# A four-layer vision stack on one core: a separate tile for the second product of the output projection, another order at the beginning and the end, and norms of both token blocks side by side

## The chip, the core and the metric

The kernel runs on one core of a Trainium2 chip. The core has a matrix engine (TensorE, PE in the profile, with weight loads as PEld), a vector engine (VectorE, DVE), an activation engine (ScalarE, ACT), GpSimd (POOL) and SyncE (SP), which issues the transfers. The metric is device time in microseconds, the median of several runs. All data are 32-bit floats.

## The reference

The input has 4 images of 512 channels and 32x32 pixels, 1024 tokens each. Four layers follow each other:

```python
# layer 0: attention with 8 heads of 64, residual
qkv = xs @ Wp.T + bp;  attn = softmax(q k * 64**-0.5);  x = res @ Wo.T + bo + xs
# layer 1: linear attention with softplus features, residual
wval = Qf (Kf^T V) * norm;  x = x + gamma * wval
# layer 2: LayerNorm over the channels of each token, attention with one head of 512, residual
xn = (xf - mu) * rsqrt(var + 1e-5) * norm_w;  x = x + (softmax(q k * 512**-0.5) v) w_proj + b_proj
# layer 3: GroupNorm, attention with 4 heads of 128, residual
```

The mean and the variance of layer 2 are taken for each token over its 512 channels.

## The kernel before

**Layout.** An image (in the code "batch" b) lies as x with channels on the 128 partitions, in 4 chunks c, and tokens along the free dimension, in two blocks tb of 512. A 128x128 by 128x512 product appears as two records of PE in the trace, and as two weight loads. Products go to accumulation tiles `acc` (4 buffers of one bank) or to `two_tile` (2 buffers of two banks).

**Strassen-like products.** `seven_products` computes a 2x2 block product with seven instead of eight block products p1 to p7 (Winograd's form). It needs four sums of the inputs (`sum_inputs`, on VectorE) and four sums of the weights (`sum_weights`, on GpSimd, L704 to L707: s[0] first, then s[1], which reads s[0], s[2], and s[3], which reads s[1]). p6 uses s[1], p7 uses s[2], p5 uses s[0], p3 uses s[3]; p1 and p2 need no sums. In each group of outputs they run in the order p1, p1, p2, p2, then p6, p7, p6, p5, p4, p7, p3, p5, p4, p3.

**Who calls `sum_weights`.** `block_sums` (tile `ws` of 128x256 operands, for the query and key projections), `project_v` (tile `ws` of 128x512 operands, from the weights `w` or `wqkv`), `output_sums` (tile `os`), and layer 2 itself, for the score product of its single head: there the "weights" are the queries (L1815, tile `qs`, 128x1024 operands, the fourth sum written over `q`). In layer 2 the program calls it for `qs` first, then calls `project_v`, then `one_head`, which uses `qs`.

**Order on the engines.** The order of PE is the order of the program (`manual_schedule`, L1673). A scheduler sets the order of the other engines from its own model of when things are ready, with some links written out: `tc.issue_after(i)` puts an instruction behind another one in the order, `soon()` raises a priority. Each engine runs its own queue in order. `pieces` is a list of small jobs of a neighbouring layer or batch that are put between products, one per `slot()`; `idle` is an empty job, which leaves one slot for something to come ready. `later` holds jobs that come due after some steps of attention.

**Output projection.** `project_out` (L1071) is a seven-product form too, over half a token block. Its first product goes into tile ps[1], ScalarE copies it to d (L1112, tile `ou`), and the second product accumulates on the same tile, so that it waits for the copy. `finish` adds the tile to x (L1101), and in the last layer stores it. Parts `second`, `third` and `fourth` are due with some steps in between in layer 0 and one right after another in layer 3.

**LayerNorm.** `layer_norm` (L1563) for one token block: `add` sums the four chunks of x on VectorE to a row tile; `center` multiplies it with a 128x128 matrix of ones (L1580, so that each partition holds the sum), subtracts the mean from four chunks (L1582), squares on ScalarE and adds (L1591); `spread` multiplies the squares with ones (L1596), takes the root and the reciprocal (L1599); `scale` multiplies the four chunks (L1604). For batches 2 and 3 both blocks are done in the previous batch of layer 2 (L1817), in slots of `project_v` and `one_head`.

**Beginning and end.** The first transfers are x and the query weights chunk by chunk, then the key weights, the second token block, the value weights (L586 to L593). In the last projection, `end_program` (L1135), the products of three of four chunks are made for all four outputs, then the verdict on the range of the denominators (`end()`, L1661), then the last chunk for outputs 0, 2, 1, 3, each added to x and stored (L1065).

## Time and profile before

| | us |
|---|---|
| median of 3 runs | 2415.14 (2414.91 to 2416.72) |
| profiled execution | 2416.26 |
| its span | 2414.5 |
| PE busy | 2398.0 (99%) |
| VectorE busy | 1503.3 (62%) |
| ScalarE busy | 702.0 (29%) |
| GpSimd busy | 247.8 (10%) |
| transfers | 110.15 MB, mean 46 GB/s |

Layer 0 with layer 1 in its slots runs to about 906 us, layer 2 to about 1566, layer 3 to the end. In the views, a line of the timeline gives start, duration, engine, line of the code, operation, output and input tiles, shapes and count, and in brackets the idle time before it with what ended it. A line of the waits gives who waited for whom, the sum in us, the number of waits and the longest. The duration of a single PE record is that of a pipelined product; the distance between starts is what it costs.

### The profile page before, as it was taken

How to read it: one execution, taken by the hardware profiler on the slowest of the kernel's cores; microseconds unless marked ns; L12 is line 12 of the kernel's file. 1: busy time of each engine (PE TensorE's matmuls, PEld its weight loads, DVE VectorE, ACT ScalarE, POOL GpSimd, SP SyncE). 2: the span in 40 equal slices, each digit the busy share in tenths (PEclk: the TensorE clock that was granted, in tenths of full speed). 3: DMA queues.
4: the chain of work that ended last, by engine and by line, in shares of the span. 5: the costliest groups of instructions: out<-in, count | busy, mean ns of one | idle time of the engine just before them, and what ended most of it. 6: DMA issues, size and time to landing. Idle time of an engine off the chain costs nothing.

```text
span 2414.5 us, 24620 instructions
## 1 busy us (share of the span) xinstructions
PE 2398.0 (99%) x10002; PEld 1197.7 (50%) x10002; DVE 1503.3 (62%) x1820; ACT 702.0 (29%) x866; POOL 247.8 (10%) x240
## 2 busy tenths in 40 slices
PE   9999999999999999999999999999999999999999
PEld 4544534453445344544646445455556446455653
DVE  4578577757875789695676765654463554445344
ACT  1454154415531653230302202013221330331132
POOL 4001100110020001102102020111020001002000
PEclk9999999999999999999999999999999999999999
DMA  5001220212021213112001020110010001001001
GB/s 188 2 18 36 57 80 11 61 31 80 19 62 64 99 37 104 64 54 78 1 9 70 13 87 0 61 70 18 35 70 0 23 31 53 0 35 35 0 26 41
DMA packets 44485, 110.15 MB, mean 46 GB/s; under 512 B 3687, under 2 KB 19559, under 8 KB 41422
## 3 DMA queue, kind: packets, MB, share of 16 engines
q1 hardware_dynamic: 44366, 108.52, 13.4%
q8 instruction: 80, 1.31, 0.2%
q14 instruction: 39, 0.32, 0.0%
HBM read 73.69 MB, written 33.77 MB: 45 GB/s over the span
## 4 chain that ended last, share of the span: by engine, by line
PE 97%; DVE 2%; ACT 0%; issue 0%; DMA 0%; SPq 0%; DVEq 0%; ACTq 0%
PE acc L716 19%; PE acc L841 12%; PE acc L976 9%; PE acc L991 9%; PE sc L945 9%; PE sc L940 9%; PE acc L1299 8%; PE acc L848 8%; PE acc L1093 7%; PE acc L1027 1%; PE upd L1534 1%; PE acc L1465 1%; PE feat L1389 0%; PE out L1141 0%; PE feat L650 0%; PE kv L1514 0%
## 5 line engine op out<-in xcount | busy, mean ns | idle before, releaser
L950 ACT ACTIVATE pt<-sc 128x1024 f32<-128x1024 f32 x384 | 379.6, 1022 | 531.6 <-PE sc L945 304.1
L959 DVE TENSOR_TENSOR sum<-sum,pt 128x1024 f32<-128x1024 f32 x256 | 314.5, 1229 | 159.6 <-ACT pt L950 147.0
L976 PE MATMUL acc<-pt,v 64*64 64x512 f32 x2048 | 245.7, 591 | 0.0
L940 PE MATMUL sc<-q,k 64*64 64x512 f32 x2048 | 243.8, 591 | 1.1 <-ACT pt L950 1.1
L991 PE MATMUL acc<-pt,v 128*128 128x512 f32 x512 | 240.8, 594 | 0.0
L945 PE MATMUL sc<-q,k 128*128 128x512 f32 x512 | 239.8, 593 | 0.0
L716 PE MATMUL acc<-t,ws 128*128 128x512 f32 x384 | 173.9, 593 | 0.0
L704 POOL TENSOR_TENSOR ws<-wqkv 128x256 f32<-128x256 f32 (+1 forms) x40 | 39.3, 982 | 1294.2 <-PE acc L1027 513.3
L956 DVE TENSOR_TENSOR sum<-pt 128x1024 f32<-128x1024 f32 x64 | 78.0, 1219 | 137.4 <-ACT pt L950 137.4
L991 PEld LDWEIGHTS acc<-pt,v 128*128 128x128 f32 x512 | 96.6, 190 | 125.3 <-issue 121.6
L945 PEld LDWEIGHTS sc<-q,k 128*128 128x128 f32 x512 | 96.8, 190 | 116.2 <-issue 92.9
L976 PEld LDWEIGHTS acc<-pt,v 64*64 64x64 f32 x2048 | 76.7, 133 | 144.0 <-issue 141.2
L940 PEld LDWEIGHTS sc<-q,k 64*64 64x64 f32 x2048 | 76.3, 133 | 141.8 <-issue 133.0
L716 PEld LDWEIGHTS acc<-t,ws 128*128 128x128 f32 x384 | 72.7, 190 | 88.0 <-issue 87.5
L755 ACT COPY v<-acc 128x512 f32<-128x512 f32 x24 | 14.1, 586 | 305.1 <-PE acc L841 305.1
L687 DVE RECIPROCAL rd<-acc 128x512 f32<-128x512 f32 (+1 forms) x25 | 83.8, 3353 | 29.1 <-PE acc L1027 29.1
L1093 PE MATMUL acc<-ot,wo 128*128 128x256 f32 x360 | 86.7, 383 | 4.1 <-ACT ou L1112 3.4
L755 ACT COPY q<-acc 128x512 f32<-128x512 f32 x40 | 23.5, 586 | 223.6 <-PE acc L716 223.6
L841 PE MATMUL acc<-ws,t 128*128 128x256 f32 x384 | 87.1, 380 | 0.0
L848 PE MATMUL acc<-qs,w 128*128 128x512 f32 x192 | 86.5, 592 | 0.0
L848 PE MATMUL acc<-q,ln 128*128 128x512 f32 x192 | 86.4, 593 | 0.0
L1093 PEld LDWEIGHTS acc<-ot,wo 128*128 128x128 f32 x360 | 67.2, 190 | 28.8 <-issue 10.3
(307 smaller groups left out, 3375.6 us busy)
## 6 DMA issues: line engine op xcount, KB each, us to landing
home<-x SPq DMA_DIRECT2D x8, 2048.0 KB
x<-home SPq DMA_DIRECT2D x8, 2048.0 KB
rds<-quotients SPq DMA_DIRECT2D x32, 256.0 KB
squares<-squares SPq DMA_DIRECT2D x32, 256.0 KB
out<-x SPq DMA_DIRECT2D x32, 256.0 KB
rds<-quotients SPq DMA_DIRECT2D x7, 1024.0 KB
x<-in_x SPq DMA_DIRECT2D x3, 2048.0 KB
v<-squares SPq DMA_DIRECT2D x12, 512.0 KB
```

What stands on the lines that cost most here:

```text
L687: nc.vector.reciprocal(rd, ps)
L716: nc.tensor.matmul(ps, lhsT=w[:, m, :], rhs=x[:, m, :], start=start, stop=stop, skip_group_check=True)
L841: nc.tensor.matmul(ps[:, bass.ts(r, C // 2)], lhsT=x[:, m, bass.ts(2 * o + r, P)], rhs=w[:, m, :], start=(start and r == 0), stop=stop, sk ...
L848: nc.tensor.matmul(ps, lhsT=x[:, m, bass.ts(o, P)], rhs=w[:, m, :], start=start, stop=stop, skip_group_check=True,)
L940: nc.tensor.matmul(ps[half(h), s, :], lhsT=key(g, i)[half(s), half(h)], rhs=q[qb][half(s), g, :], start=True, stop=True,)
L945: nc.tensor.matmul(ps[:, s, :], lhsT=key(g, 2 * i + s), rhs=q[qb][:, g, :], start=True, stop=True)
L950: exps.append(nc.scalar.activation(pt, ps, AF.Exp, scale=scale).ins)
L959: adds.append(nc.vector.tensor_tensor(acc, acc, pt, ALU.add).ins)
L976: nc.tensor.matmul(outs[qb, g][r][half(s), :], lhsT=v[i // 2][half(r), i % 2, g * P + s * hd : g * P + (s + 1) * hd], rhs=pt[half(r), s, : ...
L991: nc.tensor.matmul(outs[qb, g][0], lhsT=v[j // 2][:, j % 2, bass.ts(g, P)], rhs=pt[:, s, :], start=(j == 0), stop=(j == NT - 1),)
L1093: nc.tensor.matmul(ps[i][:, bass.ts(o, n)], lhsT=w[:, m, bass.ts(o, P)], rhs=t[:, m, :], start=(start and m + o == 0), stop=(stop and m == ...
L1299: nc.tensor.matmul(ps[i, o], lhsT=w[m][:, bass.ts(o, P)], rhs=t[m], start=(start and m == 0), stop=(stop and m == 3), skip_group_check=True,)
```

## The change

Six things change. (1) The first query weights come in two transfers, the first of 128 columns; the second token block comes before the key weights, and these in two halves. (2) Six products of the ones matrix with itself stand first in the order of PE, into a tile that nothing reads. (3) In `sum_weights` the first sum is put behind the second sum of the call before (`seconds`), and the third behind the second of its own. (4) The second product of `project_out` gets a tile of its own, ps[2]; `finish` adds that and d to x. (5) In `end_program` the first three chunks are multiplied for outputs 0 and 2 alone before the verdict, then the last chunk of these, then outputs 1 and 3 whole; the last output is added and stored in halves. (6) For batches 2 and 3, `layer_norm_pair` takes the place of two `layer_norm`: the sums of both blocks are made by products with 32 columns of ones, into rows 0 to 31 and 32 to 63 of one tile, ScalarE scales them (or takes the root, with one reciprocal for both), and two transfers by way of DRAM spread the two rows over the partitions; the mean is then added from memory and not from the product's tile.

```diff
--- before.py
+++ after.py
@@ -585,11 +585,15 @@
     x_tile(0)
     for c in range(NC):
         nc.sync.dma_start(xs[0][:, c, :TB], xin[0, :, c, :TB])
-        nc.sync.dma_start(wqkv0[:, c, :C], wview[:, c, :C])
+        for o in ((0, P), (P, C)) if c == 0 else ((0, C),):
+            nc.sync.dma_start(wqkv0[:, c, slice(*o)], wview[:, c, slice(*o)])
     cols = const.tile([P, NCOLS], F32, name="cols")
     nc.sync.dma_start(cols, d["cols"])
-    nc.sync.dma_start(wqkv0[:, :, C : 2 * C], wview[:, :, C : 2 * C])
     nc.sync.dma_start(xs[0][:, :, TB:], xin[0, :, :, TB:])
+    for o in ((C, C + 2 * P), (C + 2 * P, 2 * C)):
+        nc.sync.dma_start(wqkv0[:, :, slice(*o)], wview[:, :, slice(*o)])
     nc.sync.dma_start(wqkv0[:, :, 2 * C :], wview[:, :, 2 * C :])
     loaded0 = load_bias(d["bv0"], d["wo0n"], v_tiles()[:2])
     wo0 = load_wo(d["wo0"])
@@ -657,6 +661,8 @@
     joined, summed = [], []
+    seconds = []
     def tick():
         for item in later:
             item[0] -= 1
@@ -701,9 +707,12 @@
     def sum_weights(s, w):
-        nc.gpsimd.tensor_tensor(s[0], w(1, 0), w(1, 1), ALU.add)
-        nc.gpsimd.tensor_tensor(s[1], s[0], w(0, 0), ALU.subtract)
-        nc.gpsimd.tensor_tensor(s[2], w(0, 0), w(1, 0), ALU.subtract)
+        with tc.issue_after(seconds[-1]) if seconds else nullcontext():
+            nc.gpsimd.tensor_tensor(s[0], w(1, 0), w(1, 1), ALU.add)
+        seconds[:] = [nc.gpsimd.tensor_tensor(s[1], s[0], w(0, 0), ALU.subtract).ins]
+        with tc.issue_after(seconds[0]):
+            nc.gpsimd.tensor_tensor(s[2], w(0, 0), w(1, 0), ALU.subtract)
         nc.gpsimd.tensor_tensor(s[3], w(0, 1), s[1], ALU.subtract)
         return s
@@ -1062,12 +1071,6 @@
             with tc.issue_after(exps[-1]):
                 nc.scalar.activation(xv, xv, AF.Identity, bias=bo[:, g : g + 1])
-        def finish(qb, o, ps):
-            xv = x[:, o, bass.ts(qb, TB)]
-            nc.vector.tensor_tensor(xv, ps, xv, ALU.add)
-            if last:
-                nc.sync.dma_start(xout[b, :, o, bass.ts(qb, TB)], xv)
         def project_out(qb):
@@ -1108,13 +1111,14 @@
                         xv(i, tb),
                     )
-            mult(1, w(0, 0), inputs(0, 0), stop=False)
+            mult(1, w(0, 0), inputs(0, 0))
             nc.scalar.copy(d, view(ps[1]))
             sum_inputs(t, inputs)
             def second():
-                mult(1, w(0, 1), inputs(1, 0), start=False)
-                finish(0, 0, 1, xv(0, 0))
+                mult(2, w(0, 1), inputs(1, 0))
+                finish(0, 0, 2, xv(0, 0), d)
                 mult(6, os[1], t[1])
                 add(6, d)
@@ -1136,20 +1140,32 @@
             ot = ots.pop(qb)
             two = [two_tile("out") for _ in range(NC // 2)]
-            for o in range(NC):
-                for c in range(NC - 1):
+            def mult(o, cs):
+                ps = two[o // 2][:, o % 2, :]
+                for c in cs:
                     nc.tensor.matmul(
-                        two[o // 2][:, o % 2, :], lhsT=wo[:, c, bass.ts(o, P)], rhs=ot[:, c, :],
-                        start=(c == 0), stop=False,
+                        ps, lhsT=wo[:, c, bass.ts(o, P)], rhs=ot[:, c, :],
+                        start=(c == 0), stop=(c == NC - 1),
                     )
+                if c < NC - 1:
+                    return
+                n = 2 if o == NC - 1 else 1
+                for h in range(n):
+                    ts = bass.ts(h, TB // n)
+                    xv = x[:, o, qb * TB : (qb + 1) * TB][:, ts]
+                    nc.vector.tensor_tensor(xv, ps[:, ts], xv, ALU.add)
+                    nc.sync.dma_start(xout[b, :, o, qb * TB : (qb + 1) * TB][:, ts], xv)
+            early, late = range(NC - 1), (NC - 1,)
+            mult(0, early)
+            mult(2, early)
             end()
-            for o in sorted(range(NC), key=lambda o: o % 2):
-                ps = two[o // 2][:, o % 2, :]
-                nc.tensor.matmul(
-                    ps, lhsT=wo[:, NC - 1, bass.ts(o, P)], rhs=ot[:, NC - 1, :],
-                    start=False, stop=True,
-                )
-                finish(qb, o, ps)
+            mult(0, late)
+            mult(2, late)
+            mult(1, range(NC))
+            mult(3, range(NC))
@@ -1607,6 +1623,72 @@
         return [add, center, spread, scale]
+    def layer_norm_pair(b, tiles):
+        t = {"sq": []}
+        x = lambda tb, c: xs[b][:, c, bass.ts(tb, TB)]
+        n = P // 4
+        def add():
+            t["s"] = [row_tile("s") for _ in range(NTB)]
+            for tb, s in enumerate(t["s"]):
+                nc.vector.tensor_tensor(s, x(tb, 0), x(tb, 1), ALU.add)
+                for c in range(2, NC):
+                    nc.vector.tensor_tensor(s, s, x(tb, c), ALU.add)
+            t["all"] = work.tile([P, NC, TB], F32, tag="rds", name="norms")
+        def sums(parts):
+            ps = two_tile("lnsums")[:, 0, :]
+            for tb, s in enumerate(parts):
+                nc.tensor.matmul(
+                    ps[tb * n : (tb + 1) * n, :], lhsT=ones[:, :n], rhs=s, start=True, stop=True
+                )
+            return ps[: NTB * n], row_tile("lnrow")[: NTB * n]
+        def spread(i, row):
+            home = dram.tile([NTB, TB], F32, tag="norms", bufs=2, name="norms")
+            nc.sync.dma_start(home, row[0 : NTB * n : n])
+            nc.sync.dma_start(t["all"][:, i : i + NTB, :], home.partition_broadcast(P))
+        def means():
+            ps, row = sums(t.pop("s"))
+            nc.scalar.activation(row, ps, AF.Copy, scale=-1.0 / C)
+            spread(0, row)
+        def center(tb):
+            xn = tiles[tb]
+            for c in range(NC):
+                nc.vector.tensor_tensor(xn[:, c, :], x(tb, c), t["all"][:, tb, :], ALU.add)
+            for c in range(NC):
+                sq = row_tile("sq")
+                nc.scalar.activation(sq, xn[:, c, :], AF.Square)
+                if c == 0:
+                    t["sq"].append(sq)
+                else:
+                    nc.vector.tensor_tensor(t["sq"][tb], t["sq"][tb], sq, ALU.add)
+        def deviations():
+            ps, row = sums(t.pop("sq"))
+            nc.scalar.activation(row, ps, AF.Sqrt, bias=eps[: NTB * n], scale=1.0 / C)
+            nc.vector.reciprocal(row, row)
+            spread(NTB, row)
+        def scale(tb):
+            for c in range(NC):
+                v = tiles[tb][:, c, :]
+                nc.vector.scalar_tensor_tensor(
+                    v, v, col("nw2", c), t["all"][:, NTB + tb, :], ALU.mult, ALU.mult
+                )
+        return [
+            add, means, lambda: center(0), lambda: center(1), deviations,
+            lambda: scale(0), lambda: scale(1),
+        ]
     affine = {}
@@ -1671,6 +1753,12 @@
     with tc.manual_schedule(engines={mybir.EngineType.PE}):
+        ps = acc_tile()
+        for _ in range(6):
+            nc.tensor.matmul(ps[:, :P], lhsT=ones, rhs=ones, start=True, stop=True)
         bo0 = []
@@ -1814,9 +1902,9 @@
             places = [halves[:, 0], halves[:, 1], third, pair(q[1], 0)]
             sum_weights(places, lambda i, j: pair(q[i], j))
             if 0 < b < B - 1:
-                (add0, *n0), (add1, *n1) = [layer_norm(b + 1, tb, after) for tb in range(NTB)]
+                norm = layer_norm_pair(b + 1, after)
                 pieces.extend([
-                    add0, n0[0], idle, n0[1], n0[2], add1, n1[0], idle, n1[1], n1[2],
+                    norm[0], idle, norm[1], idle, idle, *norm[2:4], idle, norm[4], idle, idle, *norm[5:],
                 ])
             elif b > 0:
                 first = chunks_tile("ot", "gn")
```

In the built program, the order of PE differs only at these places. That of VectorE differs where instructions were added or removed, and in the first part of layer 2. The order of GpSimd differs throughout.

## The prediction

> **What bounds the kernel now.** I read the page first (busy times), then the waits of TensorE, then the timeline of each place that the change touches. The page says that TensorE is busy nearly all the time, and the waits say how little there is to win:

> ```profile
> PE 2398.0 (99%) x10002; PEld 1197.7 (50%) x10002; DVE 1503.3 (62%) x1820; ACT 702.0 (29%) x866; POOL 247.8 (10%) x240
> ...
> PE acc L716 <- DMA wqkv<-in_wqkv: 4.7, 1, 4.7
> PE acc L1093 <- ACT ou L1112: 3.4, 5, 0.7
> PE sc L940 <- ACT pt L950: 1.1, 4, 0.3
> PE acc L1093 <- DVE ot L1060: 0.7, 1, 0.7
> ```

> All waits together are 10.4 us; the last product ends at 2408.5 us, and 6.0 us of tail follow. So any instruction taken from TensorE counts in full, and any operand that becomes late counts in full. The beginning is also slow: the weight load before 9.88 us takes 0.34 us, those after it 0.19 us.

> ```profile
> 9.10 0.34 PEld L716 LDWEIGHTS acc<-x,wqkv 128*128 128x128 f32 x1 [0.52 <-issue]
> 9.88 0.19 PEld L716 LDWEIGHTS acc<-x,wqkv 128*128 128x128 f32 x1 [0.45 <-issue]
> ```

> The 32 records of L716 from 4.70 to 21.04 us take 16.3 us, where 32 x 0.429 = 13.7 is the later pace: 2.6 us are lost to a slow clock. The windows at the end show the clock falling again (columns: length of the stretch; busy time and count of PE, PEld, DVE, ACT, POOL; granted clock; share of DMA; GB/s):

> ```profile
> 2411.00:2412.00 1.00, 0.00 (x0) 0.00 (x0) 0.00 (x0) 0.00 (x0) 0.00 (x0) 1.00 0.14 43
> 2412.60:2412.80 0.20, 0.00 (x0) 0.00 (x0) 0.00 (x0) 0.00 (x0) 0.00 (x0) 0.95 0.00 0
> 2412.80:2413.00 0.20, 0.00 (x0) 0.00 (x0) 0.00 (x0) 0.00 (x0) 0.00 (x0) 0.50 0.32 82
> ```

> It drops from 1.00 to 0.50 at about 2412.8, 4.3 us after the last product.

> The place that decides is layer 2. Timeline of GpSimd (start, duration) and of TensorE in batch 1:

> ```profile
> 1124.22 1.72 POOL L704 TENSOR_TENSOR ws<-w 128x512 f32<-128x512 f32 x1
> ...
> 1127.12 1.27 POOL L705 TENSOR_TENSOR ws<-ws,w 128x512 f32<-128x512 f32 x1
> ...
> 1146.66 2.35 POOL L704 TENSOR_TENSOR qs<-q 128x1024 f32<-128x1024 f32 x1 [16.93 <-DVE q L748]
> 1148.96 2.35 POOL L706 TENSOR_TENSOR qs<-q,q 128x1024 f32<-128x1024 f32 x1
> 1151.27 2.35 POOL L705 TENSOR_TENSOR qs<-qs,q 128x1024 f32<-128x1024 f32 x1
> ...
> 1145.63 7.07 PE L841 MATMUL acc<-w,ln 128*128 128x256 f32 x32
> 1152.53 1.02 PE L1580 MATMUL lnsums<-s,ones 128*128 128x512 f32 x2
> ```

> The value projection starts at 1145.63 and wants its weight sums `ws` at 1152.5; they were made at 1124 to 1130, long before. The sums `qs` of the queries, wanted only by the scores after it, are made at 1146.66 to 1156.1, when the last query is joined.

> **The change part by part.** The sum is made against the profiled execution's own 2416.26 us (span 2414.5), which is 1.1 us above the median, 2415.14. 0.2% is 4.8 us, about what a measurement of this kernel can tell from no change.

> *Order of the weight sums.* `sum_weights` now ties its first instruction behind the second one of the call before it. In the code the call for `qs` stands before the one in `project_v`, so in the built program GpSimd runs, in each batch of layer 2: `qs` first, second, third, `ws` first, `q` fourth, `ws` second, third, fourth. The hoist of `ws` to 1124 is gone. TensorE's product with the second `ws` (p6) waits for it, and everything stands behind that in its queue. From the start-to-start times of the rows: 2.4 + 2.3 + 2.3 for three `qs`, 1.2 for `ws` first, 2.3 for `q`, 1.3 for `ws` second, 0.1 for the signal, together 11.9 us after the join. Batch 1: 1146.66 + 11.9 = 1158.6 against 1152.5, a stall of 6.1. Batch 2: 1295.61 + 11.9 against 1301.45, 6.1. Batch 3: 1444.56 + 11.9 against 1450.6, 5.9. Batch 0 has pieces of layer 1 ahead of p6 (996.74): 985.41 + 11.9, 0.6. Together +18.7. The third sum follows 1.3 later, before p7 needs it 1.7 later. Bounds: 17.5 with rows 2% shorter; 22 if every `ws` row takes 1.72, as one did beside a busy VectorE. In layers 0 and 3 the new order costs nothing: `ws` then waits for block sums 2 and 3, but 14 products, over 20 us, lie between these and p6.

> *The clock in these stalls.* Three stalls of 6 us outlast the 4.3 us after which the clock fell at the end, and at the beginning it took 5.2 us of work to return. Upper bound: 5.2 us at half pace, 2.6 each, 7.7 in all; lower bound 0, if it doesn't fall. The stall passes the 4.3 us by only 1.8, and both delays are single samples, so I take a little over half: +4.5. [...]

> *Beginning.* The first weights are 64 KB instead of 256: at the 358 GB/s of the stretch from 3 to 4 us that is up to 0.5 us off the first wait, at least 0 (the input is as large as before): -0.25. Six 128x128 products of `ones` run from 1.2 us. They are 12 records of 0.21 (a quarter of the 0.855 us spacing) to 0.34 (a weight load each), so they end at 3.8 to 5.3, at worst 0.6 us past the old start. If the clock rises 5.2 us after the first work, at 6.4, the real products from 4.45 lose 1.0 instead of 2.6: -1.6. Bounds -2.6 and 0, with +0.6 for the late end. [...] The second token block now loads before the key columns, and these come in halves: first half at about 14.3 (the third megabyte was in at 12.9, the fourth at 15.6), two sums of 0.73 to 1.7 on GpSimd, 17.7 at the latest; TensorE needs them at 4.45 + 13.7 + 1.0 = 19.2. Nothing. SP issues two more transfers, 0.5 us each, before loads that have 2 us or more in hand.

> *Second product in its own tile.* Four of the five 3.4 us waits on L1112 (the copy of `ou`, one in each batch of layer 3) go: 4 x 0.68 = -2.7. Next late would be `oi` (L696), done at 1710.3 where the product would reach it at 1715.2: covered. The fifth, at 919.6, goes but the product then waits for `ot` (L1060) until 922.1 as before: 0. The new addition of `d`, 15 x 0.6 us on VectorE, lies in its idle gaps of about 1 us between these products, save in batch 3 of layer 0, where VectorE runs without a gap from 929 to 966 and TensorE already waits 0.28 us for it: +0.4 (0 to 1.5, the reordered softplus there included).

> *Norms side by side* (batches 2 and 3). Before: 4 products of 0.86 each. After: 2 pairs of 32 columns. Such a pair is L1252: the product before it ends at 1228.17, the next starts at 1229.24, 1.07. So 2 x (3.43 - 2.14) = -2.6; nothing if the pairs don't overlap. One reciprocal of 3.35 us fewer per batch. The rows now go through DRAM: four small transfers each, while SP has nothing from 1131 to 1233. From reciprocal to use the like path takes 5.4 us (1233.1 to 1238.5). The centering waits for it on VectorE, with the joins of the products queued behind; by the rows it lands within 1 us of where VectorE gets there, and TensorE has some 0.7 us before the second pair needs the squares: 0, to +2 a batch if it is 3 us late.

> *End.* Products are as many and end at the same time: six before the verdict reach 2399.3, when the last `ot` (2398.0) is ready. Two outputs leave earlier, the last one in halves, with one more issue of 0.4 us and 128 KB less at the end: -0.2 (-0.6 to +0.3).

> Sum: 18.7 + 4.5 - 0.25 - 1.6 - 2.7 + 0.4 - 2.6 - 0.2 = +16.25. 2416.26 + 16.25 = 2432.5; less the 1.1 to the median, **2431.4 us**.

> **The rivals.**
> 1. *The clock holds in the stalls.* For it: a 4.3 us delay is one sample. Without the 4.5: 2426.9. Still slower.
> 2. *The norms' rows land late* and VectorE, waiting at the centering, holds the joins: +2 a batch for 3 us late, 2435.4. Against it: the like transfer took 3.7 us every time for 512 KB.
> 3. *The other side: the weight sums are in time.* If `ws` second is ready by 1152.5, neither stall nor clock loss exists, and the rest, -6.95, gives 2408.2, faster. It decides if GpSimd does in 5.9 us what its rows put at 11.9. For it: GpSimd spans are rough. Against it: four sums start 2.3 us apart, each using the engine in turn, in all four batches.
> 4. *The first products don't raise the clock*: +1.6, 2433.0.

> **How the numbers follow.** The forecast with rival 4 within it 0.70, rival 1 0.14, rival 2 0.10, rival 3 0.04, larger losses that I have not seen 0.02. All but rival 3 are slower by more than 0.2% (above 2420.0); the lower bounds of all terms together give +8.5, 2423.6, the upper ones +29, 2444. The range 2425 to 2438 leaves out rival 3, the tail of rival 2 and the corners. Slower 0.95, same 0.01, faster 0.04.

> **What would show it.** TensorE's waits gain a row for the value projection's product on GpSimd's `ws`, three of about 6 us and one of under 1.5. The weight loads after each go to 0.34 us where the clock fell. The L1112 wait keeps one case of 0.7 or none, and the first products run before 4 us. A wait list without GpSimd refutes the forecast; a wait of the second pair of norm products on VectorE of over 1 us speaks for rival 2.

## The result, and the profile after

The changed kernel takes 2433.8 us (2432.6 to 2436.5) against 2415.15 us before: 1.0077 times as long, 95% interval 1.0064 to 1.0090. The forecast was 2431.4, in a range of 2425 to 2438. The profiled execution took 2434.46 us, its span is 2432.7, that is 18.2 more than before.

The waits of TensorE after the change (who waits for whom; sum in us, number, longest):

```profile
PE acc L850 <- POOL ws L713: 17.8, 4, 5.8
PE acc L1096 <- DVE ot L1069: 1.7, 1, 1.7
PE sc L949 <- ACT pt L959: 1.1, 4, 0.3
PE acc L1760 <- DVE ones L629: 1.1, 1, 1.1
PE acc L1096 <- DVE oi L702: 0.2, 1, 0.2
```

The first row is new, and it is the row that the forecast named: the value projection waits for GpSimd's `ws`. The waits on the first weights (4.7) and on the copy of `ou` (3.4, five times) are gone; the new small products wait 1.1 us for their `ones`, and the first real product starts at 3.97 instead of 4.70. All in all TensorE waits more than twice as long as before: 21.9 instead of 10.4.

The place in batch 1, timeline of GpSimd and of TensorE (start, duration):

```profile
1144.70 2.35 POOL L712 TENSOR_TENSOR qs<-q 128x1024 f32<-128x1024 f32 x1 [21.74 <-DVE q L757]
1147.13 2.35 POOL L713 TENSOR_TENSOR qs<-qs,q 128x1024 f32<-128x1024 f32 x1
1149.43 2.35 POOL L715 TENSOR_TENSOR qs<-q,q 128x1024 f32<-128x1024 f32 x1
1151.74 1.26 POOL L712 TENSOR_TENSOR ws<-w 128x512 f32<-128x512 f32 x1
1152.95 2.34 POOL L716 TENSOR_TENSOR q<-q,qs 128x1024 f32<-128x1024 f32 x1
1155.25 1.26 POOL L713 TENSOR_TENSOR ws<-ws,w 128x512 f32<-128x512 f32 x1
...
1143.67 7.07 PE L850 MATMUL acc<-w,ln 128*128 128x256 f32 x32
1156.57 6.56 PE L850 MATMUL acc<-ws,w 128*128 128x256 f32 x16 [5.83 <-POOL ws L713]
1163.06 1.05 PE L1647 MATMUL lnsums<-s,ones 128*32 128x512 f32 x4
```

GpSimd stands idle for 21.74 us, starts when the last query is joined, and makes four sums over `q` and one over `w` before the `ws` that TensorE waits for. Then a second loss is seen in the same lines: the 16 records of p6 take 6.56 us, where the 32 before them took 7.07. The windows show why (columns: length; busy time and count of PE, PEld, DVE, ACT, POOL; granted clock; share of DMA; GB/s):

```profile
1153.00:1154.00 1.00, 0.00 (x0) 0.00 (x0) 0.00 (x0) 0.00 (x0) 1.00 (x1) 1.00 0.00 0
1155.00:1156.00 1.00, 0.00 (x0) 0.00 (x0) 0.00 (x0) 0.00 (x0) 1.00 (x2) 0.77 0.00 0
1158.00:1159.00 1.00, 1.00 (x4) 0.81 (x3) 0.00 (x0) 0.00 (x0) 0.96 (x1) 0.50 0.00 0
1162.00:1163.00 1.00, 1.00 (x5) 0.61 (x3) 0.00 (x0) 0.00 (x0) 0.00 (x0) 0.82 0.00 0
```

A mean clock of 0.77 in the window from 1155 says that it was 1.00 for 0.54 us and 0.50 after that: it fell at 1155.54. In the same way it returned at 1162.36. It fell in the stall, and it stayed low for 5.8 us of the work that followed.

Where the 18.2 us come from is read off the places of the same product in both timelines (starts in us):

| product | before | after | difference |
|---|---|---|---|
| first with a weight sum (query projection) | 21.04 | 18.56 | -2.48 |
| output projection on `oi`, last batch of layer 0 | 923.42 | 921.39 | -2.03 |
| value projection, layer 2, batch 0 | 986.34 | 983.81 | -2.53 |
| the same, batch 1 | 1145.63 | 1143.67 | -1.96 |
| the same, batch 2 | 1294.58 | 1300.49 | +5.91 |
| the same, batch 3 | 1443.53 | 1457.41 | +13.88 |
| last projection | 2394.01 | 2412.98 | +18.97 |
| end of the span | 2414.5 | 2432.7 | +18.2 |

The loss is made in three steps of about 8 us, one for each of batches 1 to 3 of layer 2 (+7.87, +7.97, and between the value projection of batch 3 and the last projection +5.09, which is +8.87 less the 3.78 that layer 3 gains by itself, as a run below shows). Of the other stretches, the beginning and the end are shorter, and batch 0 loses 0.6 to its own short wait.

### The profile page after: what moved, and what is told of

It is laid out like the page before. It is cut to its first block, busy times and chain, and to the rows that moved or that the text cites. A ratio compares the mean times of both kernels' runs of the same rounds, so it can differ in the third digit from the quotient of the medians.

```text
span 2432.7 us, 24733 instructions
## 1 busy us (share of the span) xinstructions
PE 2405.4 (99%) x10014; PEld 1203.1 (49%) x10014; DVE 1498.5 (62%) x1834; ACT 702.3 (29%) x866; POOL 242.2 (10%) x240
## 5 line engine op out<-in xcount | busy, mean ns | idle before, releaser
L755 DVE TENSOR_TENSOR v<-acc,v 128x512 f32<-128x512 f32 x72 | 49.7, 691 | 53.1 <-PE acc L850 53.0
```

## The experiments

The theory had two links: the order of two calls on GpSimd makes the stalls, and the stalls make the slow clock. Two experiments each take one link away, and one puts the first link alone into the kernel before. The code shown with each run holds the lines that matter, not its whole edit.

**Without the ties.**

```diff
-        with tc.issue_after(seconds[-1]) if seconds else nullcontext():
-            nc.gpsimd.tensor_tensor(s[0], w(1, 0), w(1, 1), ALU.add)
-        seconds[:] = [nc.gpsimd.tensor_tensor(s[1], s[0], w(0, 0), ALU.subtract).ins]
-        with tc.issue_after(seconds[0]):
-            nc.gpsimd.tensor_tensor(s[2], w(0, 0), w(1, 0), ALU.subtract)
+        nc.gpsimd.tensor_tensor(s[0], w(1, 0), w(1, 1), ALU.add)
+        nc.gpsimd.tensor_tensor(s[1], s[0], w(0, 0), ALU.subtract)
+        nc.gpsimd.tensor_tensor(s[2], w(0, 0), w(1, 0), ALU.subtract)
```

> The changed kernel with only the ties between the weight sums left out; every other part of the change stays. Theory (the queue position of the value projection's sums makes the stalls, and the stalls make the slow clock): TensorE's wait on GpSimd (17.8 us in all) goes, and so do the 9.1 us that the records after the three long stalls lose at half clock: 2433.8 - 17.8 - 9.1 = 2406.9 us, and TensorE's waits have no row with GpSimd's `ws` above 0.5 us. First rival (the stalls also hide something, such as the norms' rows that go through DRAM, which then come late): the sums' row goes but the norms' transfers or the centering take its place, 2 us or more a batch in batches 2 and 3, about 2411. Second rival (the loss is spread over the other parts, the sums being only where it shows): not under 2415.

Measured: 2409.5 us, 0.9976 times the kernel before (0.9967 to 0.9985). Its waits, and GpSimd and TensorE in batch 1:

```profile
PE acc L1091 <- DVE ot L1064: 1.7, 1, 1.7
PE sc L944 <- ACT pt L954: 1.1, 4, 0.3
PE acc L1755 <- DVE ones L629: 1.1, 1, 1.1
PE acc L720 <- POOL ws L709: 0.7, 1, 0.7
PE acc L720 <- DVE w L700: 0.4, 1, 0.4
```

```profile
1126.63 1.27 POOL L709 TENSOR_TENSOR ws<-ws,w 128x512 f32<-128x512 f32 x1
...
1146.17 2.36 POOL L708 TENSOR_TENSOR qs<-q 128x1024 f32<-128x1024 f32 x1 [16.92 <-DVE q L752]
...
1145.14 7.07 PE L845 MATMUL acc<-w,ln 128*128 128x256 f32 x32
1152.04 3.62 PE L845 MATMUL acc<-ws,w 128*128 128x256 f32 x16
```

`ws` is made at 1126 again, in idle time of GpSimd, and 16 records take 3.62 us. So the ties cost 24 us, and the rest of the change is a gain of 0.24%. The norms' rows through DRAM are not late without the stall (no wait on them stands in the list): the first rival is out, and the second too, since the time is under 2415. The time is 2.6 us above the 2406.9 expected, and the places say where: this kernel reaches the product on `oi` at 922.27 instead of 921.39 and loses 1.16 us more by the value projection of batch 0 (985.85 instead of 983.81). The ties had a use in both stretches. In the first it is seen: without them the scheduler lets the third sum go before the second, and at 19 us the second comes 0.7 us too late, in the row `L720 <- POOL ws`. Of the second stretch 0.4 stand in the row on VectorE's `w`; what makes the rest was not followed.

**The ties alone in the kernel before** (the same lines, added to it).

> The kernel before with only the ties between the weight sums put in. Theory: the stalls of the value projection (17.8 us) with the slow clock after three of them (9.1 us) come whole, and nothing else changes: 2415.1 + 26.9 = 2442.0 us. Rival (ties and the other parts act on one another, for example the sums are late only since the two norms' work moved): under 2430.

Measured: 2440.3 us, 1.0105 (1.0090 to 1.0121). TensorE in batch 1:

```profile
1144.09 7.07 PE L846 MATMUL acc<-w,ln 128*128 128x256 f32 x32
1151.00 1.02 PE L1585 MATMUL lnsums<-s,ones 128*128 128x512 f32 x2
1157.00 9.09 PE L846 MATMUL acc<-ws,w 128*128 128x256 f32 x32 [4.99 <-POOL ws L709]
```

The ties alone bring the stalls and the slow clock; the rival is out. From the value projection of batch 0 to the last projection this kernel loses 23.8 us; the span grew by 23.3, since 2.1 us were won before that stretch and 1.6 were lost behind it, which I did not follow. It is less than 26.9, because the product for the norm (1151.00) still stands in front of the stall here, which shortens it to 4.99 in two batches, and because the clock returned earlier in the work: in batch 1, 32 records take 9.09 instead of 7.07, a loss of 2.0 where the changed kernel loses 2.85.

**Work inside the stall.**

```diff
+            ps = two_tile("fill")[:, 0, :]
+            for _ in range(6):
+                nc.tensor.matmul(ps, lhsT=ones, rhs=bv1, start=True, stop=True)
```

> The changed kernel, and in batches 1 to 3 of layer 2 six further products of 128x128 by 128x512, whose result nobody reads, between the value projection's first 32 records and the product that waits for GpSimd: 6 x 0.857 = 5.1 us of work inside a stall of 5.8 us. Theory (the clock halves since TensorE stands idle): TensorE's wait there falls to about 0.7 us each, but the product starts no earlier; the clock stays at 1.00, the 16 records after it take 3.4 us instead of 6.5, 3.05 us less in each of three batches: 2433.8 - 9.1 = 2424.7 us. Rival (the slow 6.8 us come from something other than idleness, such as GpSimd's and VectorE's traffic at that moment): 2433.8 us, with the clock at 0.50 as before. Third possibility (the added products themselves get in the way): above 2434.

Measured: 2425.9 us, 1.0043 (1.0028 to 1.0058). TensorE in batch 1, and one window of it:

```profile
1143.78 7.07 PE L854 MATMUL acc<-w,ln 128*128 128x256 f32 x32
1150.69 5.31 PE L834 MATMUL fill<-bv,ones 128*128 128x512 f32 x12
1156.69 3.72 PE L854 MATMUL acc<-ws,w 128*128 128x256 f32 x16 [0.69 <-POOL ws L713]
1160.34 1.05 PE L1652 MATMUL lnsums<-s,ones 128*32 128x512 f32 x4
```

```profile
1158.00:1159.00 1.00, 1.00 (x7) 0.87 (x6) 0.21 (x1) 0.00 (x0) 1.00 (x1) 1.00 0.00 0
```

The product starts as late as before (1156.69 against 1156.57), but the clock stays at 1.00 and the 16 records take 3.72. By the distances between batches the gain is 2.83, 2.93 and 2.97 us: the slow clock costs 8.7 us in the changed kernel, and idleness of TensorE is its cause. (The 9.1 in the expectations was read from the length of records; the starts are the better measure, and give 8.7. The medians differ by 7.9.)

**The ties kept, the two calls in the other order.** In layer 2 the sums of the value weights, moved into a function of their own, are called for ahead of those of the queries.

```diff
+            ws = value_sums(hv, wpool.tile([P, NC, C], F32, tag="wo", name="ws"))
             sum_weights(places, lambda i, j: pair(q[i], j))
```

> The changed kernel with all ties, but in layer 2 the call that makes the value projection's sums stands ahead of the call for the queries' sums. Theory (not the ties as such, but that they fix the order of two calls the wrong way round): the sums `ws` are made before the last query is joined, stalls and slow clock are gone as without ties, 2406.9 us, within 1 us of the version without ties. Rival (a tie costs by itself, GpSimd then starting each sum late): `ws` still late by 1 us or more in each batch, 2410 or above.

Measured: 2409.6 us, 0.9974 (0.9964 to 0.9984), the same as without ties. A tie by itself costs nothing that these runs can tell; what costs is that it fixes two calls in an order in which the later one is needed first. There was one surprise in its trace, at the wait for `ot` in the last batch of layer 0:

```profile
916.10 2.75 PE L1100 MATMUL acc<-ot,wo 128*128 128x256 f32 x12
920.52 1.13 PE L1100 MATMUL acc<-ot,wo 128*128 128x256 f32 x4 [1.67 <-DVE ot L1073]
921.82 7.10 PE L1100 MATMUL acc<-oi,os 128*128 128x256 f32 x24 [0.17 <-DVE oi L702]
```

```profile
921.00:922.00 1.00, 0.83 (x5) 0.44 (x4) 1.00 (x3) 0.00 (x0) 0.00 (x0) 0.95 0.25 31
923.00:924.00 1.00, 1.00 (x4) 0.73 (x3) 1.00 (x3) 0.00 (x0) 0.00 (x0) 0.50 0.99 279
```

The same 24 records take 5.42 us in the kernel before (from 923.42) and in the changed one (from 921.39). Here the clock was low from 921.90 to 925.31, after a standing of only 1.67 and 0.17 us. This is taken up below.

**Each of the other parts alone**, in the kernel before. First the tile of its own:

```diff
-                mult(1, w(0, 1), inputs(1, 0), start=False)
-                finish(0, 0, 1, xv(0, 0))
+                mult(2, w(0, 1), inputs(1, 0))
+                finish(0, 0, 2, xv(0, 0), d)
```

> The kernel before with only the second product of the split output projection in a tile of its own. Theory (the copy of `ou` made TensorE wait, and nothing is late behind it): the five waits of 3.4 us in all on that copy go, and each of the four batches of layer 3 gains 0.7 to 0.95 us: 2.7 to 3.8 us, 2415.4 - 3.3 = about 2412.1. Rival (the next operand, `oi` or VectorE's new addition, takes the wait's place): TensorE's waits show a new row of 2 us or more and the time stays at 2415.

Measured: 2413.5 us, 0.9990 (0.9981 to 0.9999). From the value projection of batch 3 to the last projection it takes 946.70 instead of 950.48 us, 3.78 less, 0.95 for each batch of layer 3. Between the product on `oi` and the value projection of batch 0 it takes 63.59 instead of 62.92, 0.67 more, which the kernel without ties loses too. In layer 0 TensorE now waits once, for `ot` and 1.7 us, instead of twice for 0.7 us, for `ou` and for `ot`. The time is 1.4 us above the 2412.1 expected; these 0.67 are part of it, and the rest was not followed.

Then the norms side by side (the new function and its use in batches 1 and 2 of the loop, nothing else):

> The kernel before with only the norms of two token blocks side by side, in batches 2 and 3 of layer 2, and without any stall in the value projection that could give the rows time to come through DRAM. Theory (4 products of 0.86 us become 2 pairs of 1.07): 2 x 1.29 = 2.6 us less, 2412.8. Rival (the norms' rows land late once the stall doesn't hide them): a wait of TensorE or VectorE at the centering of 1 us or more a batch, 2415 or above.

Measured: 2413.5 us, 0.9991 (0.9982 to 1.0001). The distance from batch to batch is 147.88 instead of 148.95, twice: 2.14 us. No wait stands at the centering:

```profile
1150.96 3.62 PE L841 MATMUL acc<-ws,w 128*128 128x256 f32 x16
1154.51 1.05 PE L1631 MATMUL lnsums<-s,ones 128*32 128x512 f32 x4
1155.49 3.72 PE L841 MATMUL acc<-ws,w 128*128 128x256 f32 x16
```

And the beginning (the loads and the small products):

> The kernel before with only the new beginning: six small products first, the first weights in two pieces, the second token block ahead of the key columns. Theory (small products let the clock rise earlier): the product with the second weight sum, at 21.0 us before, starts 1.5 to 2.5 us earlier. From the run without ties: this needs the sums of the key columns in time, which land later in this order, and without ties the second sum of GpSimd stands third, so 0.7 us of it is lost again at 19 to 20 us: start at 19.0 to 20.0, and 2415.4 - 1.3 = 2414.1 in all. Rival (the beginning gives what the changed kernel showed, 2.0 us, by itself): 2413.4. A time can't tell these two; the place of the product and the wait on `ws` can.

Measured: 2415.35 us, 1.0001 (0.9991 to 1.0010). The product with the second weight sum starts at 19.95:

```profile
3.84 15.50 PE L720 MATMUL acc<-x,wqkv 128*128 128x512 f32 x32
19.95 7.13 PE L720 MATMUL acc<-t,ws 128*128 128x512 f32 x16 [0.61 <-POOL ws L709]
```

As the theory said, it waits for the second sum, which the scheduler puts third. The time itself tells nothing at this size.

**The changed kernel without ties and with the old order of loads.**

```diff
-        for o in ((0, P), (P, C)) if c == 0 else ((0, C),):
-            nc.sync.dma_start(wqkv0[:, c, slice(*o)], wview[:, c, slice(*o)])
+        nc.sync.dma_start(wqkv0[:, c, :C], wview[:, c, :C])
...
```

The rest of the edit puts the other loads back into their old order and takes out the ties.

> The changed kernel without the ties and with the loads of the beginning in the order of the kernel before, the small first products kept; everything else as changed. Theory (the key columns, loaded late, made the second weight sum late by 0.7 us in the run without ties): no wait on GpSimd's `ws` at all, the first product with a weight sum at 18.3 to 19.3 us instead of 19.8, and 2409.5 - 0.7 = 2408.8 us. Rival (the order of the loads itself saves time at the first product, 3.85 instead of 4.26 to 4.70): 2409.5 or above.

Measured: 2408.8 us, 0.9972 (0.9962 to 0.9983): the lowest median of all, but not to be told from the 2409.5 without ties. The theory was half right. GpSimd is in time, and something else is late at the same place:

```profile
4.28 14.80 PE L716 MATMUL acc<-x,wqkv 128*128 128x512 f32 x32 [0.23 <-DMA wqkv<-in_wqkv]
19.95 7.10 PE L716 MATMUL acc<-t,ws 128*128 128x512 f32 x16 [0.86 <-ACT q L762]
```

With the other order the second weight sum held the product to 19.8; here ScalarE's copy into `q` holds it to 19.95. That the time came out at the 2408.8 expected is luck, then: the place that was to give the 0.7 us did not give it.

**How much idle time does the clock bear?** The same products in the stall as above, but two or four instead of six.

> As the run with six further products in the stall, with two of them: 1.7 us of work, whose result nobody reads, then 4.1 us of standing idle. [...]

> As the run with six further products in the stall, with four of them: 3.4 us of work, whose result nobody reads, then 2.4 us of standing idle. [...]

Measured: 2434.4 us with two (1.0081, 1.0064 to 1.0098), and 2428.9 with four (1.0056, 1.0039 to 1.0073). With four, batches 1 and 2:

```profile
1150.64 3.60 PE L834 MATMUL fill<-bv,ones 128*128 128x512 f32 x8
1156.65 5.41 PE L854 MATMUL acc<-ws,w 128*128 128x256 f32 x16 [2.42 <-POOL ws L713]
...
1306.32 3.60 PE L834 MATMUL fill<-bv,ones 128*128 128x512 f32 x8
1312.32 3.72 PE L854 MATMUL acc<-ws,w 128*128 128x256 f32 x16 [2.41 <-POOL ws L713]
```

Two stalls of the same length, and only the first is followed by slow records: 16 records take 5.41 us, and the clock reads 0.50 in the window from 1158 to 1159; in batch 2 they take 3.72. With two products the granted clock of the four runs is 0.995 to 0.996, as in the changed kernel; with four it is 0.998 to 0.999, with six 1.00. My estimate had been that two products buy next to nothing, 2431 to 2435 us, and that with four the clock falls in some executions and not in others, 2424.7 to 2433.8; both times lie within. What decides between two stalls of 2.4 us was not shown.

## Why the prediction came out right, and where its sum was off

All differences of this section are those of the profiled executions, taken from starts.

| step | predicted | measured |
|---|---|---|
| stalls at `ws` | 6.1 + 6.1 + 5.9 + 0.6 = +18.7 | 6.00 + 6.00 + 5.77 + 0.58 = +18.35 |
| clock in the stalls | +4.5 (0 to 7.7) | 2.85 + 2.94 + 2.98 = +8.8 |
| beginning | -1.85 | -2.03 |
| own tile in layer 3 | -2.7 | -3.78 |
| layer 2's start | +0.4 | -0.50 |
| norms side by side | -2.6 | -2.14 |
| end | -0.2 | -0.77 |
| sum | +16.25 | +17.9, and +18.2 in the span |

The clock's row is the time that the first 16 records behind each stall take, from start to start, less the same time in the run with six added products. The 0.3 us that the rows leave open lie in the same records: in batch 1 they take 3.65 us behind a wait even at full clock, and 3.55 without a wait.

That the sum is off by less than 2 us is in part luck. The clock's term was 4.3 us too small; the gains of the beginning, the own tile, layer 2's start and the end were together put 2.7 us too small, and made up for more than half of that.

*Order of the weight sums*: the mechanism, the place and the size were right. The stalls are the distance from the start of the value projection to p6, less the same distance in the kernel without ties (in batch 1, 12.90 less 6.90). Reading the order of GpSimd's queue and adding the rows of the six sums up to `ws` second gave the stall to 2%.

*The clock in these stalls*: the step that was mis-sized. I took "a little over half" of an upper bound of 7.7; the loss is 8.8 and lies above the bound. Both halves of the step failed. The bound took 5.2 us, a single sample from the beginning, as the longest time of slow work. Behind the stall of batch 1 it was 5.79 (1156.57 to 1162.36), and 5.98 and 6.07 behind those of batches 2 and 3. And the share came from doubt whether the clock would fall at all, since the stall passes the 4.3 us seen at the end by only 1.8. But these 4.3 us are no fixed delay: in the changed kernel the clock fell 4.8 to 5.0 us after the last product before each stall, and with the ties alone, in batch 1, at most 3.0 us after it (that product ends at 1152.02, and the clock reads 0.50 in the whole window from 1155). Behind all three stalls of the changed kernel, of 5.6 to 5.8 us, it fell, and the slow work was of nearly the same length.

*Beginning*: the mechanism was right, but a single profile can't give its size. The same old beginning put the product with the second weight sum at 21.04, 19.52, 21.15 and 19.45 us in four profiles (before, ties alone, own tile, norms). In three of these the weight loads were read: the first that takes 0.19 us stands at 9.88 (before), 10.85 (own tile) and 7.43 us (norms), so the clock returns at another time in each. The changed beginning with ties put it at 18.50 to 19.31 in five. On the mean the gain is 1.5 us, 20.29 less 18.78; without ties (19.78 and 19.95) it is 0.4. The key columns, priced at "Nothing", do cost: they land so late that the second sum must come second, and only the ties see to that.

*Own tile*: right in kind, 0.95 instead of 0.68 a batch; the row of the wait is 0.68, the distance of starts shrinks by 0.95. The +0.4 was priced for the new tile alone: by itself it costs 0.67 there, and the ties alone gain 0.6 in the same stretch (62.33 instead of 62.92), which I had not seen.

*Norms*: 1.07 saved a batch, not 1.29. Around the first pair, from the start of the value projection to the product on `w` behind it, 15.53 us became 14.99: a pair costs 1.18 in its place, where I read 1.07 from another line.

*End*: the last product ends 5.25 us before the end of the span instead of 6.02.

*Two bounds*: rows 2% shorter take about 1 us off the 18.7 and give 17.7, not 17.5, and the upper sum of +29 holds nothing for late rows (up to +4 by rival 2's price). The forecast doesn't rest on either.

*The rivals.* Rival 1, the clock holds, is refuted by the windows, and the run with six added products shows what it would have been. Rival 2, the rows land late, is refuted in the changed kernel and also without any stall. Rival 3, the sums in time, did not occur; made to occur, it gives 2409.5 where the prediction's rest gave 2408.2. Rival 4, the first products don't raise the clock, is refuted by the weight loads: in five profiles with the small products the first that stands alone with 0.19 us starts at 5.53 to 6.74 us (mean 6.0), in three without them at 7.43 to 10.85 (mean 9.4).

## What to carry to other kernels

A helper called from several places that ties each call behind the one before also fixes the order of calls that had nothing to do with each other: list what lies between the new position of each tied instruction and its first reader, and have the call that is needed first come first. Price a new stall of TensorE with its clock: the gap itself, and the slow work behind it, which lasted 5.8 to 6.1 us in the changed kernel and cost 2.85 to 2.98 us a stall. Where an operand can't be had sooner, work can be put into the gap: with 5.3 us of it, and 0.7 us left idle, the clock stayed at 1.00; with 3.6 us of it, and 2.4 us left idle, it fell in batch 1. Here it was work that nobody reads, and work that was to be done anyway should do the same at no cost, which was not run.

## What the runs showed of the hardware

*Idle time of TensorE and the clock.* Before the product on `ws` TensorE stood idle for 5.83, 5.84 and 5.62 us in the changed kernel, and the clock fell each time. With the ties alone, in batch 1, it was 4.99 us, and the clock fell. With four added products it was 2.42 us in batch 1 and 2.41 in batch 2: the clock fell in the first, and in the second 16 records took 3.72 us, as at full clock. With six it was 0.69 and 0.70 us, and 16 records took 3.72 both times. The surprise is the run with the two calls exchanged: a wait of 1.67 us was followed by a fall and cost 1.7 us more (24 records in 7.10 instead of 5.42 us). In six other profiles with the same wait of 1.67 us (changed, without ties, own tile, old loads, four and six products) the clock read 1.00 in all windows from 900 to 1000 us. So waits of the same length, 1.67 and 2.4 us, were seen with a fall and without one; what decides was not shown.

*Work until the clock returned.* Behind the stalls of the changed kernel TensorE worked for 5.79, 5.98 and 6.07 us at 0.50 before the clock returned. At the beginning the first weight load that stands alone with 0.19 us came 3.4 us earlier on the mean with the small products first (five profiles) than without them (three).
